# Two tiles of a two-layer kernel: norms and half the bias steps moved from ScalarE to VectorE, and another planned order

## The chip, the cores and the metric

The kernel runs on one core of a Trainium2 chip. A core has five engines, each with its own instruction queue that runs strictly in order: TensorE (PE, matrix products), VectorE (DVE), ScalarE (ACT, table functions), GpSimd (POOL) and SyncE (SP, here the queue from which all transfers are issued). [...] The metric is device microseconds of one execution, the median of several runs.

## The reference

Two layers work on x of 2 sequences x 2048 positions x 256 features. Layer 0 normalizes x, runs a state-space block (projection, a convolution of four taps, softplus, a scan over time with 16 states for each of 512 channels, gating, projection, a residual and a GELU feed-forward), and multiplies it with the SiLU of a gated network whose weights and activations are quantized to 4-bit floats. Layer 1, the part that the change touches, is cut here to what matters:

```python
xn = layernorm(x)
# attention over the two sequences (their axis is the attended one)
s = out_proj(softmax(q @ k.T * scale) @ v) + out_proj_bias
h = xn                                    # three low-rank-corrected blocks
for blk in range(3):
    y = qlora_linear(h, 2*blk)            # x W^T + bias + (x A^T) B^T
    y = layernorm(y) * gamma + beta
    y = gelu(y)
    h = qlora_linear(y, 2*blk+1) + h
x = x + s * silu(h)
```

All arithmetic is float32.

## The kernel before

**Tiling.** The positions of a sequence are cut into 8 pieces of T = 256; with B = 2 sequences that gives 16 steps (j, b). A step has the stages HEAD (norm, input projection, convolution, softplus), QUANT (`fp4_half`, the gated network), SCAN (16 states, each one: ScalarE makes four 128x256 `decay` tiles, VectorE multiplies, scans 1028 columns and multiplies again, TensorE adds the transposed result into a `bank_y`), and TAIL (norm and feed-forward, then `x1`). After the second sequence's step of each j comes SECOND: `second(j, g, x1)` for g = 0, 1 does layer 1 on 128 positions of both sequences. There are 16 such tiles. The two of the last j have streams of their own, `e0` and `e1`, with other buffers and PSUM banks (`bank_m`, `bank_y`, `bank_h`, `bank_f`), since nothing else is left by then; all others are `s0` and `s1`.

**A tile of layer 1.** `second` (line 1100) takes the statistics of x1 on VectorE, gets the inverse root on GpSimd (`inverse_root`, line 705: a tensor_scalar and a power), normalizes on ScalarE, transposes on TensorE, does the attention (over two elements it is a sigmoid), and then walks three blocks k = 0, 1, 2. A block is: TensorE makes `py`; ScalarE squares it with a running sum, twice (the weights had their mean taken out, so the mean of squares is the variance); GpSimd makes `y`; ScalarE scales twice; TensorE transposes; ScalarE applies Gelu; TensorE adds the second product to `hb`; ScalarE adds the bias, in two halves m (k = 2 applies SiLU instead). The lines, of before:

```python
rec.scalar.activation(yn[:, bb, :], py[:, bb, :], AF.Square, accum_out=sq[:, bb : bb + 1])
y = inverse_root(st, sq, B, 1.0 / D, EPS, f"f{nm}_{k}")
rec.scalar.activation(yn[:, bb, :], py[:, bb, :], AF.Copy, scale=y[:, bb : bb + 1])
```

**What sets the order.** No operation is issued where it is written. `Recorder` keeps all of them with what they read and write, and a planner in the program's build (`order`, `forward`, `backward`) walks them with a cost for each (`cost`, line 104), a delay from one engine's end to another's start (`SEEN`, `TAIL`), the number of buffers of every tag, and a price for switching ScalarE's function table (`SWITCH`). `forward` always issues the ready operation with the highest key. The first keys come from the step number, a `lead` for each stage and the table `adjust` of (step, stage, shift); then each row of `passes` walks back from the end for due times and forward again with these as keys. What it finds is the order in which the instructions stand in the five queues. The chip doesn't see the planner's times: it sees only the queues and their semaphores. Since the whole plan follows from these numbers, a changed cost or shift moves instructions everywhere. ScalarE's table loads are put in by the compiler wherever the next function is not in the table that is loaded, so their number follows from the order, too.

All operations are issued from one line (561), so the profile is read by the names of the tiles. `hh`, `decay`, `state`: scan. `fp_l`, `fp_h`, `h`, `hq`: quantized network. `t2k_s`, `ln_y_s`, `bank_s`: layer 1's tiles; in the last two also `bank_m`, `bank_y`, and `lnt`, `ux` and `dt` as their working tiles.

Of the kernel before, what the change touches and what calls it, by code (L numbers as in the profile page):

```python
# [8 lines left out]
F32 = mybir.dt.float32  # L9
I32 = mybir.dt.int32  # L10
BF16 = mybir.dt.bfloat16
AF = mybir.ActivationFunctionType
ALU = mybir.AluOpType
AX = mybir.AxisListType
PSUM = bass.MemoryType.PSUM
DRAM = bass.MemoryType.DRAM

P = 128
D = 256
# [3 lines left out]
T = 256  # L23
# [13 lines left out]
EPS = 1e-5  # L37
# [4 lines left out]
class Recorder:  # L42
# [11 lines left out]
    SWITCH = 1.31  # L54

    SEEN = {"tensor": 0.055, "vector": 0.034, "scalar": 0.035, "gpsimd": 0.1, "sync": 0.07}
    TAIL = {"tensor": 0.165, "vector": 0.083, "scalar": 0.1, "gpsimd": 0.8, "sync": 1.7}

    WINDOW, COLUMNS = 3.4133, 3060
    RATE = 165e3  # L60
# [43 lines left out]
    def cost(self, engine, method, args, kwargs):  # L104
        out = kwargs.get("out", args[0] if args else None)
        n = 1
        for d in out.shape[1:]:
            n *= d
        if engine == "sync":
            return 0.52  # L110
        if engine == "gpsimd":
            if method == "memset":
                return 0.04
            return 0.7 if method == "tensor_tensor" else 0.3
        values = list(args[1:]) + list(kwargs.values())
        tiles = [v for v in values if hasattr(v, "tensor") and v is not out]
        if engine == "tensor":
            rhs = args[2] if len(args) > 2 else kwargs.get("rhs")
            if method == "transpose" or kwargs.get("is_transpose"):
                return 0.109  # L120
            if rhs.dtype == BF16:
                return 0.1 + n / 2400.0
            lhs = kwargs.get("lhsT", args[1] if len(args) > 1 else None)
            if lhs.shape[0] == 16 and lhs.offset >= 16 * lhs.ap[0][0]:
                return 0.1
            return 0.005 + 4 * n / 2400.0
        scalars = 0
        for v in tiles:
            m = 1
            for d in v.shape[1:]:  # L130
                m *= d
            scalars += m == 1 and n > 1
        if engine == "scalar":
            inside = bool(tiles) and self.space(tiles[0].tensor) == PSUM
            scalars += kwargs.get("accum_out") is not None
            return (0.05 if inside else 0.093) + 0.000833 * n + 0.1 * scalars
        if method == "tensor_tensor_scan":
            return 0.068 + 0.002083 * n
        if method == "bn_stats":
            return 0.333  # L140
        if method == "bn_aggr":
            return 0.1
        if method == "reciprocal":
            return 0.06 + 0.0066 * n
        if method == "tensor_reduce":
            n = 1
            for d in args[1].shape[1:]:
                n *= d
        if method in ("tensor_copy", "tensor_scalar", "memset") and n >= 64:
            return 0.07 + 0.00052 * n + 0.06 * scalars  # L150
        if n <= 32:
            return 0.078
        return 0.067 + 0.0010417 * n + (0.06 if method == "scalar_tensor_tensor" and scalars else 0.0)
# [47 lines left out]
    def prepare(self):  # L201
# [12 lines left out]
        for i, (engine, method, args, kwargs, stage) in enumerate(ops):  # L214
            if engine == "tensor":

                n = self.costs[i]
                lhs = kwargs.get("lhsT", args[1] if len(args) > 1 else None)
                if method == "transpose" or kwargs.get("is_transpose"):
                    self.size[i], self.table[i] = 128, 1  # L220
                elif lhs.dtype == BF16:
                    self.size[i], self.table[i] = (n - 0.1) * 2400, 2
                else:
                    self.size[i], self.table[i] = n * 2400 * lhs.shape[0] / 128, 3
            if engine == "sync":
                self.size[i] = 2 if args[0].dtype == BF16 else 4
                for d in args[0].shape:
                    self.size[i] *= d
# [28 lines left out]
    def order(self, lead, bonus, ahead, adjust=(), passes=()):  # L257

        own = {(b, k): v for b, k, v in adjust}
        key = [-o[4][0] - lead[o[4][1]] + own.get(o[4], 0.0) for o in self.ops]
        issued, end = self.forward(key, bonus, ahead)
        for unit, bonus_back, ahead_back, bonus, ahead, adjust in passes:
            key = [-x / unit for x in self.backward(unit, bonus_back, ahead_back)]
            for b, k, v in adjust:
                for i, o in enumerate(self.ops):
                    if o[4] == (b, k):
                        key[i] += v  # L270
            issued, end = self.forward(key, bonus, ahead)
        return issued, end

# [78 lines left out]
    def forward(self, key, bonus, ahead):  # L352
# [65 lines left out]
        while done < n:  # L418
# [25 lines left out]
            for name in self.first[i]:  # L444
                if name not in place:
                    t = max(t, tags[self.tiles[name]["tag"]]["free"][0][0])
            cost = costs[i]
            if best_e == "scalar" and table[i] and table[i] != now_table:
                t = max(t, free[best_e] + self.SWITCH)
                self.switched += self.SWITCH  # L450
                now_table = table[i]
# [113 lines left out]
def tile_two_layers(ctx: ExitStack, tc: tile.TileContext, a: dict):  # L565
# [139 lines left out]
    def inverse_root(stream, v, n, scale, plus, name):  # L705

        y = small.tile([P, n], F32, tag=f"ln_y_{stream.replace("e", "s")}", name=f"y_{name}")
        rec.gpsimd.tensor_scalar(y, v, scale, plus, ALU.mult, ALU.add)
        rec.gpsimd.tensor_tensor(y, y, power[:, :n], ALU.pow)
        return y  # L710

# [73 lines left out]
    wt = {}  # L785
# [78 lines left out]
    def head(b, j, xt):  # L864
# [57 lines left out]
            rec.sync.dma_start(bc[q * NS : (q + 1) * NS, :], xdbl[(2 * q + 1) * R : (2 * q + 2) * R, :])  # L922
        dt = mam.tile([P, 4, T], F32, tag="dt", name=f"dt_{nm}")
        ux = mam.tile([P, 4, T], F32, tag="ux", name=f"ux_{nm}")
        pdt = [bank("m", f"pdt_{nm}_{pr}").rearrange("p (m t) -> p m t", m=2) for pr in range(2)]
        for mm in range(2):
            for pr in range(2):
                rec.tensor.matmul(
# [171 lines left out]
    def second(j, g, x1):  # L1100
        nm = f"{j}_{g}"

        st = f"e{g}" if j == NJ - 1 else f"s{g}"
        xv = x1[:, g, :, :]
        xm = t2k(st, f"xm_{nm}").rearrange("p (b d) -> p b d", b=B)
        layer_norm(st, xm, xv, B, f"c{nm}")

        hb = bank({"s": "h", "e": "g"}[st[0]] + st[1], f"hb_{nm}").rearrange("p (c t) -> p c t", c=2)
        for c in range(2):
# [63 lines left out]
        for k in range(3):  # L1173
# [8 lines left out]
                    )  # L1182
            yn = t2k(st, f"yn_{nm}_{k}").rearrange("p (b d) -> p b d", b=B)

            sq = small.tile([P, B], F32, tag=f"ln_sq_{st.replace("e", "s")}", name=f"sq_{nm}_{k}")
            for bb in range(B):
                rec.scalar.activation(
                    yn[:, bb, :], py[:, bb, :], AF.Square, accum_out=sq[:, bb : bb + 1]
                )
            y = inverse_root(st, sq, B, 1.0 / D, EPS, f"f{nm}_{k}")  # L1190
            for bb in range(B):
                rec.scalar.activation(yn[:, bb, :], py[:, bb, :], AF.Copy, scale=y[:, bb : bb + 1])
            pt = transpose_pair(st, yn, f"e{nm}_{k}")
            yt = t2k(st, f"yt_{nm}_{k}").rearrange("p (c t) -> p c t", c=2)
            for c in range(2):
# [10 lines left out]
                    )  # L1206
            hn = t2k(st, f"hn_{nm}_{k}").rearrange("p (c t) -> p c t", c=2)
            for m in range(2):
                rec.scalar.activation(
                    hn[:, m, :], hb[:, m, :], AF.Identity if k < 2 else AF.Silu,  # L1210
                    bias=wt["odd"][:, k, m : m + 1],
                )
# [20 lines left out]
    for i, (j, b) in enumerate(order):  # L1233
# [20 lines left out]
        h = following  # L1254

    adjust = [
        (0, 0, 1.48), (0, 2, 0.93), (0, 3, -0.66), (1, 0, -1.29), (1, 1, -0.08), (1, 3, 0.49),
        (1, 4, -0.55), (2, 0, -0.28), (2, 1, 0.62), (2, 4, 0.73), (3, 0, -0.1), (3, 4, 0.51),
        (4, 0, 0.15), (4, 1, 0.67), (4, 2, 0.59), (4, 3, -1.78), (4, 4, -0.74), (5, 0, -0.51),
        (5, 2, 0.63), (5, 3, 0.09), (5, 4, 0.29), (6, 0, 0.66), (6, 1, 1.68), (6, 2, 0.9),  # L1260
        (6, 3, 0.26), (6, 4, 2.72), (7, 0, 0.63), (7, 1, -0.41), (7, 2, 0.3), (7, 4, 0.34),
        (8, 0, -0.58), (8, 1, -0.58), (8, 2, 0.45), (8, 3, 0.6), (8, 4, -0.47), (9, 0, 0.76),
        (9, 1, 2.32), (9, 2, -0.12), (9, 4, -0.53), (10, 0, 0.19), (10, 3, 2.6), (10, 4, 0.12),
        (11, 0, 0.54), (11, 1, -0.16), (11, 2, -0.01), (11, 3, -0.3), (11, 4, 1.13),
        (12, 0, -0.62), (12, 1, 0.85), (12, 2, 0.08), (12, 4, 0.47), (13, 0, 0.34),
        (13, 1, -0.42), (13, 2, -1.48), (13, 4, -0.77), (14, 0, -1.31), (14, 1, 0.5),
        (14, 2, -1.21), (14, 3, -1.46), (14, 4, 0.39), (15, 1, 1.91), (15, 2, -0.55),
        (15, 3, 1.48), (15, 4, 0.61),
    ]


    passes = [
        (110, 0.3, 0.0, 0.5, 0.12, [(9, 0, 0.01)]),
        (110, 0.3, 0.1, 0.5, 0.12, [(9, 0, 0.01)]),
        (80, 0.3, 0.0, 0.2, 0.12, []),
        (30, 0.3, 0.05, 0.5, 0.05, []),
        (20, 0.3, 0.1, 0.5, 0.12, []),
        (20, 0.3, 0.1, 0.5, 0.12, [(3, 4, 0.16)]),
    ]
    rec.issue(tc, lead=(0.28, -1.79, 0, -5.22, 1.4), bonus=366.531, ahead=0, adjust=adjust, passes=passes)  # L1280


# [46 lines left out]
```

## Time and profile before

| | us |
|---|---|
| median of 3 runs (1790.72 to 1791.84) | 1791.33 |
| the profiled execution: its own time | 1787.97 |
| the profiled execution: span, first to last instruction | 1786.2 |
| VectorE busy, of the span | 1630.4 (91%) |
| TensorE busy | 1585.8 (89%) |
| ScalarE busy | 1559.0 (87%) |
| of it 383 table loads | 491.4 |
| GpSimd busy | 233.2 (13%) |
| mean granted TensorE clock | 0.947 |

How to read it: in the groups, a row is an engine, an operation, what it writes and reads, the number of instructions, busy time and mean ns, and after the second bar the idle time just before them with what ended it. In the waits, "A <- B: 15.2, 14, 3.5" says that A's engine stood idle 15.2 us in 14 places, 3.5 at most, until B. In the timeline, a row is start, duration, engine, operation, with the idle time before it in brackets. Busy time of neighbouring instructions on one engine overlaps by some hundredths of a microsecond.

### The profile page before, as it was taken

How to read it: one execution, taken by the hardware profiler on the slowest of the kernel's cores; microseconds unless marked ns; L12 is line 12 of the kernel's file. 1: busy time of each engine (PE TensorE's matmuls, PEld its weight loads, DVE VectorE, ACT ScalarE, POOL GpSimd, SP SyncE). 2: the span in 40 equal slices, each digit the busy share in tenths (PEclk: the TensorE clock that was granted, in tenths of full speed). 3: DMA queues.
4: the chain of work that ended last, by engine and by line, in shares of the span. 5: the costliest groups of instructions: out<-in, count | busy, mean ns of one | idle time of the engine just before them, and what ended most of it. 6: DMA issues, size and time to landing. Idle time of an engine off the chain costs nothing.

```text
span 1786.2 us, 22221 instructions
## 1 busy us (share of the span) xinstructions
PE 1585.8 (89%) x7756; PEld 1193.1 (67%) x7756; DVE 1630.4 (91%) x1926; ACT 1559.0 (87%) x3324; POOL 233.2 (13%) x265
## 2 busy tenths in 40 slices
PE   7448878999989989899998999999899999998887
PEld 5336656677776768676776767767676767766665
DVE  7999999999989999999998999999998999999711
ACT  7556968899988999989998999999999998999645
POOL 1000010022122201211111021101111102020101
PEclk9669989899999999999999999999999999999989
DMA  6311111111111111212121212211111111212000
GB/s 180 92 41 45 48 43 59 42 45 46 45 48 45 48 49 48 60 36 49 41 61 38 52 43 54 54 31 53 43 60 37 48 49 44 46 36 64 2 6 12
DMA packets 62989, 86.77 MB, mean 49 GB/s; under 512 B 15095, under 2 KB 29085, under 8 KB 62878
## 3 DMA queue, kind: packets, MB, share of 16 engines
q1 hardware_dynamic: 62878, 85.37, 17.9%
q8 instruction: 60, 0.98, 0.2%
q14 instruction: 51, 0.42, 0.1%
HBM read 80.62 MB, written 4.72 MB: 48 GB/s over the span
## 4 chain that ended last, share of the span: by engine, by line
ACT 41%; PE 32%; DVE 19%; issue 5%; POOL 2%; DMA 0%; ACTq 0%; DVEq 0%
ACT L561 14%; PE bank_f L561 13%; ACT decay L561 11%; DVE hh L561 10%; PE bank_m L561 7%; ACT t2k_s L561 6%; PE bank_s L561 5%; PE bank_y L561 4%; DVE fp_l L561 3%; ACT t2k_f L561 3%; PE bank_h L561 2%; POOL ln_y_s L561 2%; ACT xc L561 1%; DVE t2k_s L561 1%; DVE fp_sc L561 1%
## 5 line engine op out<-in xcount | busy, mean ns | idle before, releaser
L561 DVE TENSOR_TENSOR_SCAN hh<-decay,hh 128x1028 f32<-128x1028 f32 x256 | 581.4, 2286 | 5.7 <-ACT decay L561 4.4
L561 ACT ACT_TABLE_LOAD x383 | 491.4, 1283 | 13.9 <-DMA xt<-in_x_dram 3.7
L561 ACT ACTIVATE decay<-dt,amat 128x256 f32<-128x256 f32 x1024 | 445.0, 500 | 6.4 <-DVE hh L561 3.3
L561 PE MATMUL bank_y<-ident,hh 128*128 128x128 f32 x2048 | 296.5, 284 | 30.8 <-DVE hh L561 30.6
L561 DVE TENSOR_TENSOR hh<-hh,bcs 128x1024 f32<-128x1024 f32 x256 | 308.4, 1210 | 15.9 <-ACT state L561 15.2
L561 DVE TENSOR_TENSOR hh<-ux,bcs 128x1024 f32<-128x1024 f32 x256 | 307.5, 1210 | 1.7 <-PE bank_y L561 1.6
L561 PEld LDWEIGHTS bank_y<-ident,hh 128*128 128x128 f32 x2048 | 248.7, 146 | 82.3 <-DVE hh L561 43.1
L561 PE MATMUL bank_f<-w_f,t2k_f 128*128 128x256 f32 x512 | 133.7, 388 | 14.1 <-ACT t2k_f L561 14.0
L561 POOL TENSOR_SCALAR ln_y_s<-ln_sq_s 128x2 f32<-128x2 f32 x48 | 36.9, 769 | 769.8 <-ACT t2k_s L561 458.1
L561 PE MATMUL bank_m<-xi,cdiag 128*128 128x256 f32 x512 | 127.0, 380 | 0.0
L561 PE MATMUL bank_f<-t2k_f,w_f 128*128 128x256 f32 x512 | 124.6, 384 | 2.5 <-ACT t2k_f L561 2.5
L561 PEld LDWEIGHTS bank_f<-w_f,t2k_f 128*128 128x128 f32 x512 | 92.8, 192 | 36.0 <-ACT t2k_f L561 23.5
L561 PE MATMUL bank_f<-w_down,hq 128*128 128x256 f32 (+1 forms) x384 | 103.7, 409 | 7.3 <-ACT hq L561 7.2
L561 PEld LDWEIGHTS bank_f<-t2k_f,w_f 128*128 128x128 f32 x512 | 94.9, 190 | 21.0 <-ACT t2k_f L561 7.1
L561 PE MATMUL bank_h<-t2k_s,w_l 128*128 128x256 f32 x360 | 95.2, 399 | 9.5 <-ACT t2k_s L561 9.2
L561 PEld LDWEIGHTS bank_m<-xi,cdiag 128*128 128x128 f32 x512 | 93.0, 190 | 14.1 <-issue 0.7
L561 DVE SCALAR_TENSOR_TENSOR fp_l<-fp_h,fp_l 128x704 f32<-128x704 f32 (+2 forms) x124 | 91.4, 737 | 7.5 <-ACT fp_h L561 6.9
L561 PE MATMUL bank_f<-ident,fp_l 128*128 128x128 f32 x292 | 54.5, 311 | 47.1 <-DVE fp_l L561 46.5
L561 PE MATMUL bank_f<-w_gate,t2k_f 128*128 128x352 f32 x256 | 92.7, 481 | 2.2 <-ACT h L561 1.1
L561 PEld LDWEIGHTS bank_f<-w_down,hq 128*128 128x128 f32 (+1 forms) x384 | 71.8, 199 | 34.1 <-issue 12.7
L561 POOL TENSOR_TENSOR ln_y_s<-ln_y_s,power 128x2 f32<-128x2 f32 x64 | 93.2, 1457 | 5.2
L561 PE MATMUL bank_f<-w_up,t2k_f 128*128 128x352 f32 x256 | 90.2, 466 | 0.0
(187 smaller groups left out, 2589.9 us busy)
## 6 DMA issues: line engine op xcount, KB each, us to landing
bcs<-bc SPq DMA_DIRECT2D x128, 512.0 KB, 4.8
xt<-in_x_dram SPq DMA_DIRECT2D x16, 256.0 KB, 2.8
out_dram<-t2k_s SPq DMA_DIRECT2D x15, 256.0 KB, 3.8
w_f<-in_ffn_w_dram SPq DMA_DIRECT2D x2, 1024.0 KB
t2k_s<-in_qweights_dram SPq DMA_DIRECT2D x6, 256.0 KB, 2.9
w_in<-in_in_proj_w_dram SPq DMA_DIRECT2D x1, 1024.0 KB
h<-in_w_gate_dram SPq DMA_DIRECT2D x6, 128.0 KB, 2.1
w_qkv<-in_qkv_w_dram SPq DMA_DIRECT2D x1, 768.0 KB
```

What stands on the lines that cost most here:

```text
L561: getattr(getattr(self.nc, engine), method)(*args, **kwargs)
```

## The change

1. For the two last tiles (`last`, streams e0 and e1): the first norm's normalization goes from ScalarE to VectorE (one tensor_scalar, subtract and multiply, for each sequence); the norms in the three blocks take `statistics` on VectorE (bn_stats and bn_aggr) instead of Squares on ScalarE, and scale with one VectorE tensor_tensor over 512 columns instead of two ScalarE copies; the scale-and-add ahead of the power goes from GpSimd to VectorE; and of the two bias steps of k = 0 and 1, the half m = 1 goes to VectorE.
2. The planner's costs: GpSimd's operations 0.69 and 0.19 rather than 0.7 and 0.3, its delay 0.3 rather than 0.8, and its operations (memset aside) start only when VectorE's current call is over; float32 products of fewer than 192 columns cost as 192; a ScalarE call with a running sum and a VectorE call that reads PSUM cost more.
3. New `lead`, `adjust`, `passes`, `bonus` and `ahead`; `adjust` in a pass may name an engine. The order of all queues differs.

In the built queues VectorE has 1972 instructions instead of 1928, ScalarE 3204 instead of 3230, among them 389 table loads instead of 383, GpSimd 262 instead of 270; TensorE's and SP's are as many as before, in another order.

```diff
-    TAIL = {"tensor": 0.165, "vector": 0.083, "scalar": 0.1, "gpsimd": 0.8, "sync": 1.7}
+    TAIL = {"tensor": 0.165, "vector": 0.083, "scalar": 0.1, "gpsimd": 0.3, "sync": 1.7}
...
-            return 0.7 if method == "tensor_tensor" else 0.3
+            return 0.69 if method == "tensor_tensor" else 0.19
...
-            return 0.005 + 4 * n / 2400.0
+            return 0.005 + 4 * max(n, 192) / 2400.0
...
-            scalars += kwargs.get("accum_out") is not None
+            scalars += 1.5 * (kwargs.get("accum_out") is not None)
...
+            if tiles and self.space(tiles[0].tensor) == PSUM:
+                return 0.067 + 0.0010417 * n + 0.06 * scalars
...
+            if engine == "gpsimd":
+                self.table[i] = int(method != "memset")
...
+            if best_e == "gpsimd" and table[i]:
+                t = max(t, free["vector"])
...
-        rec.gpsimd.tensor_scalar(y, v, scale, plus, ALU.mult, ALU.add)
+        if stream[0] == "e":
+            rec.vector.tensor_scalar(y, v, scale, plus, ALU.mult, ALU.add)
+        else:
+            rec.gpsimd.tensor_scalar(y, v, scale, plus, ALU.mult, ALU.add)
         rec.gpsimd.tensor_tensor(y, y, power[:, :n], ALU.pow)
...
-        layer_norm(st, xm, xv, B, f"c{nm}")
+        if last:
+            mv = statistics(st, xv, B, f"c{nm}")
+            y = inverse_root(st, mv[:, :, 1], B, 1.0, EPS, f"c{nm}")
+            for i in range(B):
+                rec.vector.tensor_scalar(
+                    xm[:, i, :], xv[:, i, :], mv[:, i, 0:1], y[:, i : i + 1], ALU.subtract, ALU.mult
+                )
+        else:
+            layer_norm(st, xm, xv, B, f"c{nm}")
...
+            if last:
+                mv = statistics(st, py, B, f"f{nm}_{k}")
+                y = inverse_root(st, mv[:, :, 1], B, 1.0, EPS, f"f{nm}_{k}")
+                rec.vector.tensor_tensor(
+                    yn, py, y.unsqueeze(2).to_broadcast([P, B, D]), ALU.mult
+                )
+            else:
...
+                if last and m == 1 and k < 2:
+                    rec.vector.tensor_scalar(
+                        hn[:, m, :], hb[:, m, :], wt["odd"][:, k, m : m + 1], None, ALU.add
+                    )
+                    continue
...
-    rec.issue(tc, lead=(0.28, -1.79, 0, -5.22, 1.4), bonus=366.531, ahead=0, adjust=adjust, passes=passes)
+    rec.issue(tc, lead=(2.87, -2.69, 0, -5.2, 0.74), bonus=2058732.142, ahead=0.015, adjust=adjust, passes=passes)
```

## The prediction

> **What bounds the kernel now.** I read the totals, then busy time by stage, then the waits before the last scan, then the timeline of the last two tiles. By stage (length, then each engine's busy us, granted clock, DMA share, GB/s):
>
> ```profile
> PE 1585.8 (89%) x7756; PEld 1193.1 (67%) x7756; DVE 1630.4 (91%) x1926; ACT 1559.0 (87%) x3324; POOL 233.2 (13%) x265
> ...
> 0.00:100.00 100.00, 59.42 (x256) 42.66 (x256) 86.00 (x192) 60.56 (x133) 9.62 (x32) 0.79 0.48 127
> ...
> 300.00:1600.00 1300.00, 1217.72 (x6054) 921.23 (x6053) 1248.23 (x1405) 1222.09 (x2623) 194.48 (x176) 0.97 0.18 47
> ...
> 1676.00:1717.00 41.00, 40.13 (x198) 31.43 (x196) 12.86 (x31) 25.60 (x50) 2.81 (x8) 1.00 0.00 1
> 1717.00:1740.50 23.50, 18.91 (x62) 11.10 (x63) 5.23 (x13) 9.48 (x16) 1.67 (x4) 0.78 0.03 11
> 1740.50:1786.20 45.70, 33.53 (x145) 23.66 (x144) 5.63 (x11) 24.48 (x66) 5.30 (x12) 0.94 0.03 12
> ```
>
> VectorE's last scan product ends at 1675.2 us. Up to 1676 it idles only 69 us: 14 in the first 100, 52 between 300 and 1600, where ScalarE idles 78. So time before 1675 is VectorE's work plus what the order makes it wait. From 1676 to 1717 TensorE is full (40.1 of 41). After 1717 nobody is full: two tiles walk one chain from engine to engine. The waits of VectorE and ScalarE before 1676 (us, times, longest):
>
> ```profile
> DVE hh L561 <- ACT state L561: 15.2, 14, 3.5
> ...
> DVE fp_l L561 <- ACT fp_h L561: 5.8, 7, 3.1
> DVE hh L561 <- ACT decay L561: 4.4, 6, 1.8
> ...
> DVE xi L561 <- PE bank_m L561: 2.7, 1, 2.7
> ...
> DVE ln_m_m L561 <- POOL ln_y_m L561: 2.5, 3, 1.4
> ...
> DVE ln_m_f L561 <- POOL ln_y_f L561: 1.8, 2, 1.2
> ```
>
> ```profile
> ACT t2k_s L561 <- POOL ln_y_s L561: 9.7, 6, 3.6
> ```
>
> All waiting for GpSimd's roots is thus 4.3 us on VectorE and 9.7 on ScalarE: the whole purse that better planning of GpSimd can open there. Two groups price the rest:
>
> ```profile
> L561 ACT ACT_TABLE_LOAD x383 | 491.4, 1283 | 13.9 <-DMA xt<-in_x_dram 3.7 <-PE bank_h L561 2.3 <-DVE hh L561 1.9
> ...
> L561 POOL TENSOR_TENSOR ln_y_s<-ln_y_s,power 128x2 f32<-128x2 f32 x64 | 93.2, 1457 | 5.2
> ```
>
> GpSimd's power takes 0.69 us in the tail, 1.46 on average. In the tail, ScalarE in one step of tile e0:
>
> ```profile
> 1755.25 0.38 ACT L561 ACTIVATE t2k_s<-bank_m 128x256 f32<-128x256 f32 x1
> ...
> 1757.74 0.47 ACT L561 ACTIVATE t2k_s<-bank_m,ln_y_s 128x256 f32<-128x256 f32 x1
> 1759.57 0.38 ACT L561 ACTIVATE lnt<-bank_y 128x256 f32<-128x256 f32 x1 [1.35 <-PE bank_y L561]
> ...
> 1760.30 0.48 ACT L561 ACTIVATE t2k_s<-bank_m,ln_y_s 128x256 f32<-128x256 f32 x1
> 1761.42 1.02 ACT L561 ACTIVATE t2k_s<-bank_m,l_bet,l_gam 128x256 f32<-128x256 f32 x2 [0.64 <-PE bank_m L561]
> ```
>
> The second half of e0's scaling stands behind e1's Square, which waits for TensorE: 2.1 us lost in the queue, not in arithmetic.
>
> **The change part by part.** The sum is made against the profiled execution: span 1786.2, its own time 1787.97, 3.4 below the median 1791.33 of the three runs. I apply the difference to the median. "Work ahead" below is the built queue, each instruction at its group's mean less the overlap with its neighbour.
>
> *Tail, the norms.* Removed from ScalarE: 12 Squares (0.38 + 0.20), 12 scalings (0.47), 4 normalizations (0.59), 4 bias steps (0.47), together 17 us; from GpSimd 8 tensor_scalars (0.19). Added to VectorE: 12 statistics (0.41), 12 aggregates (0.17), 8 small scale-and-add (about 0.15, as the 128x44 row at 0.18), 6 scalings (0.68, the row of bank_s + x at 128x512), 4 normalizations (unseen; 0.27 for a 128-wide one with a scalar, 0.475 from PSUM at 256: I take 0.40), 4 bias steps (0.475), less two 0.15: some 16 us, in a stretch where VectorE is busy 5.23 of 23.5 and 5.63 of 45.7. Per norm the chain itself doesn't shorten: old 0.84 + 0.09 + 0.96 + 0.1 + 0.82 = 2.8; new 0.75 + 0.29 + 0.15 + 0.69 + 0.69 and four hand-overs = 2.8. What goes is the queueing on ScalarE. e0's projections end at 1740.5, 1754.7 and 1768.3: 14.2 and 13.6 apart, while TensorE's work for both tiles in a step is 2 x (0.31 + 1.72 + 0.6 + 1.72) = 8.7. Bounds: only the halved bias steps count (4 x 0.36 = -1.4), or both steps fall to TensorE's 8.7 and the front gains 2.6: -13. Following the new queues from the end of e0's first projection: scaled at 2.65 (1.05 + 0.15 + 0.7 + 0.7 with hand-overs), transposed 3.3, Gelu 4.3, second product 6.0, bias 6.5; then TensorE still has e1's projection (1.7) and the rest of e1's output product (1.3) ahead of e0's next: 11.5; the next step likewise gives about 10.5. That is -6, of which half a microsecond per step may go in hand-overs. To this come 1.7 to 2.6 at the front, where VectorE normalizes right after the former tile's product instead of handing to ScalarE (1721.7 to 1723.9 today). Against it: a third Silu/Gelu alternation puts the last load (1.28) after TensorE's last product; the scaling of e0's first norm stands in front of e1's two last attention adds, so these wait out GpSimd's 0.69; TensorE's clock is 0.78 here. I take -7.
>
> *Between the last scan and 1717.* In the new order 37.5 us of TensorE work stands from the last scan's transposes to the end of the FFN; today 33.0, but TensorE starts it 3.5 late. 0 to +4.5; I take +1, since TensorE would start at once.
>
> *The order, VectorE.* Its work ahead of the last scan product is the same (1595.1 against 1594.6 us). So before 1675 only its idle time can move.
>
> *The order, start.* SP now sends the gate weights first and x second: x is one issue (0.5) later, covered by the weights' quantization on VectorE. 41.8 us of VectorE work stand before the first scan (36.6 before) and 20.2 of ScalarE's before its decay (25.3): more filler, an earlier decay. The 14.0 idle is 3.4 unavoidable (DMA and launch). Bounds 0 and -10; I take -3, the two stalls of xi (2.7) and fp_h (3.1) half gone.
>
> *The order, table loads.* 389 instead of 383, five more before the last decay, one in the tail: 5 x 1.283 = +6.4 on ScalarE, and its work ahead of the middle tiles' decays is 5 to 11 us more. ScalarE idles 78 us in that stretch, which may cover it: 0 to +10, I take +3.
>
> The trace has the next ACTIVATE 1.29 after a load starts (1745.67 to 1746.96). [...]
>
> *The order, GpSimd.* Cost figures come nearer to the rows (0.69 and 0.19, and a wait for VectorE). Yet the room on ScalarE between the last Square and the first scaling has the same median, 3.5 us, in both orders. Bounds 0 and -14 (4.3 + 9.7); I take -2. Shape edits (the slice of pdt) change nothing in any queue.
>
> Sum: -7 + 1 - 3 + 3 - 2 = -8: span about 1778, median 1783.3.
>
> **The rivals.** *A, slower: ScalarE falls behind the scans.* It already waits 45.6 us for scans before it can copy a state, and VectorE waits 15.2 + 4.4 for state and decay. With five more loads and up to 11 us more work ahead of the decays, that wait is where the middle breaks. Doubled, it is +19.6: 1803. It decides from a growth of 8. For it: 78 us of ScalarE idle is only 6%; against: its surplus is back to 3.0 us at the last decay.
>
> *B, no difference: the tail doesn't pay.* Chains are equally long, TensorE runs at a low clock, the last load is exposed: tail -2, and start and loads cancel: 1789 to 1791.
>
> *C, a larger gain.* Most of the start's stalls and of the GpSimd waits go: -7 more and -6 more: 1770. For it: the planner's GpSimd costs were far off; against: the equal room named above.
>
> **How the numbers follow.** This kernel's runs spread 1.1 us; 0.2% (3.6 us) is about what can be told from no change. Forecast 0.45 (1776 to 1788), C 0.18, B 0.15, A 0.22. Faster: forecast and C, 0.63; same: B, 0.15; slower: A, 0.22. The range leaves out the ends of A and C: 1768 to 1799.
>
> **What would show it.** Right: the stretch from e0's first to third projection falls from 27.8 to about 22; VectorE's idle before its last scan product is 66 or less; the last product ends near 1673; after it about 105 us remain instead of 111; loads 389 at 1283 ns. Wrong: VectorE's waits for state and decay above 28 us (A); steps of the last tiles still 13 apart (B); the waits for ln_y gone and under 60 us idle (C). The forecast falls first if the middle's idle, which the order sets and no row shows, moves by more than 10 either way.

## The result: slower by half a per cent

The changed kernel takes 1796.8 us, median of 15 runs (1792.19 to 1808.14), beside 1791.16 for the kernel before (15 runs, 1778.83 to 1797.57): ratio 1.0047, 95% interval 1.003 to 1.0064. The ratio is estimated from all runs and isn't the quotient of the medians: these are 5.6 us apart, and a ratio of 1.0047 is 8.4 us. Measured again later, beside other kernels (after_again below), it was 1.0061 (1.004 to 1.0082), some 11 us. The forecast was 8 us faster; the measured time lies in its range (1768 to 1799), on the other side of no change.

The profiled execution of the changed kernel took 1802.07 us (span 1800.3), 14.1 more than the profiled one of before. That is more than the medians differ by: single executions of one kernel spread by some 1% here, and the profiles show it, too, so below a size is taken from several profiles or from the times where there are any. One execution of a kernel below, before_late2, took 3271.71 us and is left out of its ratio (its median is 1785.35 without it, 1786.05 with it).

The page of after, totals and the two groups shown of before:

```profile
PE 1583.1 (88%) x7756; PEld 1198.4 (67%) x7756; DVE 1636.4 (91%) x1970; ACT 1553.3 (86%) x3286; POOL 246.3 (14%) x257
...
L567 ACT ACT_TABLE_LOAD x389 | 499.1, 1283 | 15.3 <-PE bank_h L567 2.9
...
L567 POOL TENSOR_TENSOR ln_y_s<-ln_y_s,power 128x2 f32<-128x2 f32 x64 | 95.6, 1495 | 59.1 <-DVE ln_y_s L567 54.7
```

Busy time hardly moved: the loads are as many and as long as forecast, and the mean of GpSimd's power rose by 38 ns only. The loss doesn't show in any total. By stage, after (columns as in the prediction):

```profile
0.00:100.00 100.00, 60.59 (x262) 43.74 (x262) 83.39 (x201) 55.02 (x122) 9.45 (x31) 0.83 0.48 124
...
1687.10:1736.50 49.40, 48.68 (x225) 37.51 (x223) 14.37 (x36) 27.48 (x58) 4.28 (x8) 0.99 0.00 1
1736.50:1760.10 23.60, 19.58 (x78) 12.92 (x78) 11.26 (x30) 8.96 (x15) 2.04 (x3) 0.93 0.04 12
1760.10:1800.30 40.20, 27.77 (x128) 20.59 (x128) 13.70 (x38) 14.71 (x26) 3.46 (x5) 0.96 0.04 13
```

Three stretches moved. The last scan product ends at 1687.1 instead of 1675.2. From there to the last statistics of x1 (the end of the feed-forward) it takes 49.3 us with TensorE full, where it took 41.8. From there to VectorE's last add it takes 60.6 instead of 65.7. The waits ahead of the last scan product, of VectorE and then of ScalarE:

```profile
DVE hh L567 <- ACT decay L567: 21.0, 17, 6.1
DVE hh L567 <- ACT state L567: 10.5, 11, 2.5
```

```profile
ACT t2k_s L567 <- POOL ln_y_s L567: 25.3, 7, 6.7
```

VectorE's waits for state and decay are 31.5 us (19.6 before), past the 28 that the prediction gave as the sign of rival A. A second profile of the changed kernel (after_again, below) has them shorter, under 28:

```profile
DVE hh L567 <- ACT state L567: 11.8, 12, 2.5
DVE hh L567 <- ACT decay L567: 10.9, 11, 3.4
```

What both profiles share is the wait that the change was to shorten, ScalarE's for the roots: it grew from 9.7 to 25.3 (23.0 in the second). The longest of the waits of the first profile, at GpSimd, VectorE and ScalarE:

```profile
1120.22 2.65 POOL L567 TENSOR_SCALAR ln_y_s<-ln_sq_s 128x2 f32<-128x2 f32 x1 [15.66 <-ACT t2k_s L567]
1122.95 7.75 POOL L567 TENSOR_TENSOR ln_y_s<-ln_y_s,power 128x2 f32<-128x2 f32 x1
```

```profile
1122.80 1.20 DVE L567 TENSOR_TENSOR hh<-hh,bcs 128x1024 f32<-128x1024 f32 x1
...
1125.05 0.68 DVE L567 SCALAR_TENSOR_TENSOR fp_l<-fp_h,fp_l 128x512 f32<-128x512 f32 x1
...
1126.79 1.22 DVE L567 TENSOR_TENSOR hh<-ux,bcs 128x1024 f32<-128x1024 f32 x1
1127.92 2.29 DVE L567 TENSOR_TENSOR_SCAN hh<-decay,hh 128x1028 f32<-128x1028 f32 x1
1130.13 0.67 DVE L567 TENSOR_TENSOR fp_l<-fp_l,fp_sc 128x512 f32<-128x512 f32 x1
1132.79 2.30 DVE L567 TENSOR_TENSOR_SCAN hh<-decay,hh 128x1028 f32<-128x1028 f32 x1 [2.00 <-ACT decay L567]
```

```profile
1130.73 0.84 ACT L567 ACTIVATE t2k_s<-bank_s,ln_y_s 128x256 f32<-128x256 f32 x2 [6.71 <-POOL ln_y_s L567]
```

A power of 0.69 us is out for 7.75, through six VectorE calls, and comes in where the scan of 1127.92 ends. The new planner counts on GpSimd waiting for the one call that is running. ScalarE reaches the scaling at 1124.02, 3.9 us after the last Square, and stands 6.71 us in front of it, with decays queued behind, and VectorE's next scan waits for its decay.

### The profile page after: what moved, and what is told of

It is laid out like the page before. It is cut to its first block, busy times and chain, and to the rows that moved or that the text cites. A ratio compares the mean times of both kernels' runs of the same rounds, so it can differ in the third digit from the quotient of the medians.

```text
span 1800.3 us, 22200 instructions
## 1 busy us (share of the span) xinstructions
PE 1583.1 (88%) x7756; PEld 1198.4 (67%) x7756; DVE 1636.4 (91%) x1970; ACT 1553.3 (86%) x3286; POOL 246.3 (14%) x257
## 4 chain that ended last, share of the span: by engine, by line
ACT 37%; PE 33%; DVE 21%; issue 4%; POOL 3%; DMA 1%; SPq 0%; ACTq 0%; DVEq 0%
PE bank_f L567 13%; DVE hh L567 13%; ACT L567 13%; ACT decay L567 9%; PE bank_m L567 8%; ACT t2k_s L567 5%; PE bank_s L567 5%; PE bank_y L567 5%; DVE fp_l L567 3%; POOL ln_y_s L567 3%; ACT t2k_f L567 2%; PE bank_h L567 2%; DVE t2k_s L567 1%; ACT xc L567 1%; DVE fp_sc L567 1%
## 5 line engine op out<-in xcount | busy, mean ns | idle before, releaser
L567 ACT ACT_TABLE_LOAD x389 | 499.1, 1283 | 15.3 <-PE bank_h L567 2.9
L567 PE MATMUL bank_y<-ident,hh 128*128 128x128 f32 x2048 | 286.0, 282 | 36.1 <-DVE hh L567 35.8
L567 PEld LDWEIGHTS bank_y<-ident,hh 128*128 128x128 f32 x2048 | 244.1, 145 | 84.5 <-DVE hh L567 48.0
L567 POOL TENSOR_SCALAR ln_y_s<-ln_sq_s 128x2 f32<-128x2 f32 x42 | 46.5, 1108 | 690.6 <-ACT t2k_s L567 509.8
L567 PEld LDWEIGHTS bank_f<-t2k_f,w_f 128*128 128x128 f32 x512 | 99.2, 196 | 19.1 <-ACT t2k_f L567 3.6
L567 PE MATMUL bank_f<-ident,fp_l 128*128 128x128 f32 x292 | 51.8, 307 | 46.4 <-DVE fp_l L567 37.9
```

What stands on the lines that cost most here:

```text
L567: getattr(getattr(self.nc, engine), method)(*args, **kwargs)
```

## The experiments

The planner's order is a list. Each experiment takes that list from the unchanged program and exchanges or moves single calls when it is issued (`swap` below maps a call's number to what is issued in its place), so that all other calls keep their places in the queues. The code below is shortened to its sense.

### Tail and order, each alone

```diff
+# tail_alone: order of before; the calls of the old tail replaced, e.g. for a block of e0, e1
+swap[Square(0)] = [vector.bn_stats(0)]
+swap[Square(1)] = [vector.bn_stats(1), vector.bn_aggr(0), vector.bn_aggr(1)]
+swap[gpsimd.tensor_scalar(y)] = [vector.tensor_scalar(y, variance, 1.0, EPS)]
+swap[Copy(0)] = [vector.tensor_tensor(yn, py, y)];  swap[Copy(1)] = []
+swap[Identity(m=1, k<2)] = [vector.tensor_scalar(hn, hb, bias)]
+# order_alone: order of after; the same in the other direction
```

> The order of before, kept call by call, with the last two tiles' norms, scalings and bias steps on VectorE put in at the old calls' places. Theory 1 (the order loses, the tail edit gains): about 5 us faster than before, 1786; from the statistics of x1 to the last add some 60 us instead of 65.7, all ahead of it unchanged (last scan product near 1675, then 42 us). Theory 2 (the shorter last stretch of the changed kernel comes from its new order there, the edit itself gives nothing): within 1.5 us of before, the last stretch 64 to 67.

> The order of the changed kernel, kept call by call, with the last two tiles' norms, scalings and bias steps back on ScalarE and GpSimd at the new calls' places. Theory 1: about 5 us slower than the changed kernel, so 10 to 11 us slower than before, near 1802; VectorE's waits for state and decay stay near 31 us ahead of the last scan product. Theory 2: the time of the changed kernel, 1797, since the order alone makes both the loss and the shorter last stretch.

Measured: tail_alone 1794.3 us beside 1794.74 of before, ratio 1.0005 (0.9989 to 1.0021): nothing. order_alone 1805.02, ratio 1.0074 (1.005 to 1.0097). So the loss is the order's, and theory 1 is half wrong: order_alone lost the 10 us that it forecast, but the edit of the tail isn't worth 5 us in the order of before. In the new order the two measurements of the changed kernel lie 0.27% and 0.13% below order_alone, with overlapping intervals, so no worth of the edit is shown there. The last stretch (from x1's statistics to the last add), one windows line each of before, tail_alone, before_no_root (below; old tail) and after:

```profile
1717.00:1782.70 65.70, 52.43 (x206) 34.76 (x206) 10.87 (x24) 33.97 (x82) 6.97 (x16) 0.90 0.01 4
```

```profile
1727.80:1795.90 68.10, 55.17 (x206) 37.10 (x206) 24.48 (x68) 21.30 (x38) 5.49 (x8) 0.85 0.01 4
```

```profile
1706.50:1775.30 68.80, 55.82 (x206) 37.28 (x206) 10.90 (x25) 33.96 (x82) 7.02 (x16) 0.85 0.01 4
```

```profile
1736.50:1797.10 60.60, 47.35 (x206) 33.50 (x206) 24.96 (x68) 23.68 (x40) 5.49 (x8) 0.97 0.03 9
```

ScalarE lost 12.7 us of busy time in tail_alone (33.97 to 21.30; the forecast's sum of durations was 17), and the stretch didn't get shorter. Read TensorE's column: the same 206 matmul records take 47.4 to 55.8 us, by the granted clock of 0.97 to 0.85, and the stretch is TensorE's time and 13 us in all four, whichever engine makes the norms. Two rows of tail_alone show eight products of one shape, the first time in 3.49 us, at half clock for all but the end by the clock record, the second time in 2.08:

```profile
1757.98 3.49 PE L562 MATMUL bank_y<-w_l,lnt 128*128 128x256 f32 x8
...
1770.56 2.08 PE L562 MATMUL bank_y<-w_l,ux 128*128 128x256 f32 x8 [0.62 <-ACT ux L562]
```

The clock record of the last stretch holds pieces of half clock of 3.4 us or multiples: 13.7 us in before (10.2 from 1719.3 on and 3.4 from 1773.9 on), 20.5 in tail_alone and before_no_root, 3.4 in after; the granted clocks of 0.90, 0.85, 0.85 and 0.97 in the four lines above agree. One order with one tail had 13.7 us of it in one execution and 20.5 in another. What sets the clock at half no run here shows; the longest gap of TensorE in these three stretches and in that of after is 3.0 us.

All profiles by stretch (us; the last column is TensorE's busy time in the last stretch):

| kernel | order, tail | last scan product | to x1's statistics | to the last add | TensorE |
|---|---|---|---|---|---|
| before | old, old | 1675.2 | 41.8 | 65.7 | 52.4 |
| tail_alone | old, new | 1686.0 | 41.8 | 68.1 | 55.2 |
| before_no_root | old, old | 1665.0 | 41.5 | 68.7 | 55.8 |
| before_late (see below) | old, old | 1665.8 | 53.0 | 65.1 | 51.8 |
| before_late2 | old, old | 1670.5 | 41.8 | 65.6 | 52.3 |
| before_late2_tail | old, new | 1676.3 | 41.8 | 68.4 | 55.4 |
| after | new, new | 1687.1 | 49.3 | 60.6 | 47.4 |
| after_again | new, new | 1683.7 | 48.5 | 63.6 | 50.3 |
| order_alone | new, old | 1687.1 | 48.1 | 62.3 | 50.6 |
| after_no_root | new, new | 1659.3 | 49.2 | 60.6 | 47.3 |
| after_late | new, new | 1690.6 | 49.3 | 60.7 | 47.4 |

The first column is noisy: before and tail_alone are the same up to there, and differ by 10.8. The second is not: but for before_late it is 41.5 to 41.8 in the old order and 48.1 to 49.3 in the new. The third varies with the clock, by 3 us between executions with one order and tail (65.7 and 68.7, 60.6 and 63.6). So the new order costs 6 to 8 us in the drain after the scans, and its last stretch is 2 to 8 shorter, with either tail; why TensorE's clock is higher there no run shows.

### Nobody waits for the roots

```diff
+# stream not e0, e1: GpSimd still makes y, nobody reads it
-rec.scalar.activation(yn[:, bb, :], py[:, bb, :], AF.Copy, scale=y[:, bb : bb + 1])
+rec.scalar.activation(yn[:, bb, :], py[:, bb, :], AF.Copy, scale=power[:, bb : bb + 1])
+# the same for normalize(): its product mean * y and its scale
```

> The order of the changed kernel; GpSimd still works out every root, but outside the last two tiles the calls that scale by it read a constant tile (a wrong scale), so nobody there waits for GpSimd. Theory 1 (starved roots hold ScalarE, and so the decays): ScalarE's 25 us of waits for ln_y go, VectorE's waits for state and decay fall from 31.5 to about 20, the last scan product ends 8 to 12 us earlier, time 8 to 12 us below the changed kernel (about 1786). Rival (ScalarE's five more loads and its moved work delay the decays): the waits for state and decay stay above 27 and the time falls by under 4 us.

> The order of before, with the same edit: outside the last two tiles nobody waits for GpSimd's roots (constant scale instead). Theory 1: there is less to win here, since ScalarE waits 9.7 us and VectorE 4.3 for roots: 2 to 5 us faster than before, clearly less than the same edit gives in the changed order. Rival: the same gain in both orders, whatever it is, since then the roots are not what differs.

Measured: after_no_root 1774.12 us, ratio 0.9892 (0.9869 to 0.9916); before_no_root 1779.09, ratio 0.9912 (0.9885 to 0.994). From the changed kernel's 1.0061 that is -1.7%, some 30 us; from before it is -0.9%, some 16. So the roots are what differs between the two orders: 12 to 14 us of difference, by the first or the second ratio of the changed kernel, and known to some 7 us by the intervals. Without them the new order isn't slower any more (a median 5 us lower; the two intervals overlap). The purse was larger than the expectation had it in both, and it is about what the two engines' waits for GpSimd add up to: 30.2 us in the profile of after (25.3 and 4.9; 27.6 in after_again, 28.4 in order_alone), 14.0 in that of before (9.7 and 4.3; 19.0 in tail_alone, with the same order). VectorE's waits behind them, of after_no_root (last scan product at 1659.3), then of before_no_root:

```profile
DVE hh L568 <- ACT decay L568: 5.3, 8, 1.4
...
DVE hh L568 <- ACT state L568: 2.1, 6, 0.5
```

```profile
DVE hh L562 <- ACT state L562: 8.9, 11, 2.1
...
DVE hh L562 <- ACT decay L562: 4.1, 6, 1.8
```

From 31.5 (22.7 in after_again) to 7.4 in the new order, with its 389 loads and its fuller ScalarE queue unchanged. So the loads, to which the prediction gave +3 and rival A its cause, weren't the trouble.

### The same roots' scalings later in the queue

```diff
+LATE = {16: 7, 44: 7, 49: 7, 57: 7, 58: 6, 59: 7, 65: 7, 92: 4, 93: 5, 98: 3}  # after_late: root, calls
+LATE = {16: 7, 22: 5, 29: 7, 35: 7, 100: 7}                                    # before_late
+LATE = {16: 7, 22: 5, 29: 7, 35: 7}                                            # before_late2
+order = self.later(order, LATE)  # the two scalings, and what needs them, behind so many ScalarE calls
```

> The order of the changed kernel, complete, but for ten roots of the second layer (those that GpSimd was held at for over 3.5 us in one of the runs of this order) the two scalings on ScalarE, with the transposes that read them, stand 3 to 7 ScalarE calls later, behind decays and state copies; as many table loads. Theory 1: ScalarE's waits for ln_y_s ahead of the last scan product fall from 25 us to under 6, VectorE's waits for state and decay from 31.5 (26.3 with the old tail) to under 20, time 8 to 15 us below the changed kernel: 1783 to 1790, under the kernel before. Rival (it is not the place of these scalings; the order is short of ScalarE time): the waits move to the next call, time within 4 us of the changed kernel.

> The same move in the order of before, for its five held roots (5 to 7 calls later, two table loads fewer). Theory 1: there is less to win, ScalarE waits some 10 to 14 us for five roots: 3 to 6 us faster than before. Rival: no difference in either order.

> The changed kernel itself beside the others on one chip. Both theories: 0.3 to 0.65% over before, 1796 to 1803; the long holds of GpSimd at the same roots and of the same length as in its first profile, if the order alone makes them; elsewhere and of other lengths if chance does.

Measured on one chip: after_late 1792.72 us, ratio 1.0004 (0.999 to 1.0017); after_again 1803.81, ratio 1.0061 (1.004 to 1.0082); before_late 1795.92, ratio 1.0016 (1.0004 to 1.0027). Ten pairs of calls, moved by a few places, take back 10 us, the whole loss. That is theory 1's size, though the time isn't under the kernel before, as it had it. ScalarE's waits for ln_y_s went from 23.0 (after_again) to 10.0 rather than under 6, and VectorE's for state and decay are 26.4, not under 20: the profiled execution of after_late was its slowest, at 1805.53, so its waits are no measure of the gain in the median. In after_again GpSimd's long holds came back at the same calls with the same length: 6.01, 6.61, 7.75 and 5.92 us at roots 44, 57, 65 and 92 in all three profiles of this order (the last one is of a scale-and-add, the others are powers). order_alone's row for the one shown above:

```profile
1130.98 7.75 POOL L568 TENSOR_TENSOR ln_y_s<-ln_y_s,power 128x2 f32<-128x2 f32 x1
```

So most holds belong to the order; a few others (root 49: 1.59 in after, 7.15 in order_alone and after_again) fall one way or the other. The old order has one power held so long, at root 22, 7.14 to 7.15 us in all six of its profiles.

before_late was expected to gain and lost 0.16%. Its last scan product ended 9.4 us earlier than in before (1665.8), but the next stretch took 53.0 instead of 41.8: its root 100 stands just there, and the moved calls held up TensorE's queue (busy 43.6 us of the 53.0, and 40.9 of 41.8 in before). So the next run left that one in place.

> The order of before with four held roots' scalings 5 to 7 ScalarE calls later; the fifth, which stands in the drain after the last scan, stays where it was (moving it lengthened the stretch from the last scan product to the last statistics from 41.8 to 52.9 us). Theory 1: the last scan product ends 5 to 9 us earlier than in before, as in the former run (1665.8), the drain is back at 42: 1783 to 1787, 0.3 to 0.5% faster than before. Rival: no difference (the earlier last product was chance, the spread of one kernel's profiles being about that).

> The same with the last two tiles' norms, scalings and bias steps on VectorE. If the edit of the tail is worth nothing in this order, as the run of it alone had it: the time of the run without it, within 2 us. If it is worth 5 us once the roots do not hide it: 1778 to 1782.

Measured: before_late2 1786.05 us, ratio 0.9959 (0.9944 to 0.9974), which beats both kernels, and is theory 1's size; before_late2_tail 1786.26, ratio 0.9955 (0.9938 to 0.9972). Four roots' scalings a few calls later are worth 7 us in the order of before, and the tail's edit, on top of it, nothing once more. With held roots moved in both, the new order is still behind the old one (1.0004 and 0.9959). The waits of before_late2, VectorE's and ScalarE's:

```profile
DVE hh L592 <- ACT state L592: 7.2, 10, 1.4
```

```profile
ACT t2k_s L592 <- POOL ln_y_s L592: 2.4, 4, 0.9
```

### What keeps GpSimd out

> No part of the reference: GpSimd's scale-and-add and power on 128x2 (0.19 and 0.69 us when undisturbed) are released at the start of a run of some 10 us of VectorE calls, three times for each kind of run, and nothing else goes on. Theory 1 (a run of calls with two SBUF inputs keeps GpSimd out until the run ends): the pair ends only with the run, 8 to 10 us, beside the multiplies, the scans and the scale-subtract calls, and takes 1 to 2 us beside calls with one input or one input in PSUM. Rival (GpSimd waits for the current call alone, as the new planner has it): each of the two waits at most one call, so the pair takes 2 to 3.5 us beside the multiplies and 3 to 6 beside the scans.

Measured, GpSimd's rows beside multiplies and beside bn_stats:

```profile
17.43 1.55 POOL L71 TENSOR_TENSOR y_mult<-y_mult,power 128x2 f32<-128x2 f32 x1
...
157.25 0.69 POOL L71 TENSOR_TENSOR y_stats<-y_stats,power 128x2 f32<-128x2 f32 x1
```

The rival is right: in this loop GpSimd waits for the running call alone. The pair takes 2.7 us beside multiplies and 4.8 beside scans (2.09 and 2.60), in the middle of a run of 9 to 11 us. With one input in PSUM, or bn_stats, there is no wait (0.19 and 0.69); beside a one-input multiply from SBUF to SBUF the pair takes 1.7 (0.55 and 1.11). The 7.75 above, through six calls, is more than a wait for one.

Over seven profiles (before, after, order_alone, after_again, after_late, before_late, tail_alone) the power's first chance depends on when it starts. Started 0.14 to 0.165 us into a multiply, which is where it comes when the end of the call before let in the scale-and-add, it was still out after that multiply's end in 30 of 81 cases; in 20 of these it came in only where a scan ended, after 4.9 to 8.4 us. Started 0.2 us or later into a multiply: in 0 of 109. Into a scan, at 0.14 to 0.165: 0 of 37. (A multiply here is one that writes `hh`.)

> No part of the reference: GpSimd's pair of root calls released at the start of a scan that one, two, three, four or six multiplies and then another scan follow (also eight multiplies and no scan; five multiplies first; scans alone). Theory (a power released 0.15 us into a multiply, right after a scan's end let the scale-and-add in, stays out at every multiply's end until a scan ends): the power takes about 1.2 us a multiply plus 2.2 for the scan plus 0.5: 3.8 with one, 5 with two, 7.2 with four, 9.5 with six, and 9 or more with eight and no scan. Rival (it waits for the call that is running and no other): 1.6 in all of them, 2.6 beside scans alone.

> No part of the reference: the sequence scan, multiply in place, three more multiplies, two scans, with the kernel's own tile shapes (rows of 257, a broadcast second operand), GpSimd's pair released at the first scan's start; alone, and beside ScalarE's exponentials, TensorE's transposes of the products, broadcast loads, ScalarE's earlier copies into the tiles (so that VectorE's calls carry waits), and all of them. Theory (the hold comes from the shapes and the in-place multiply): the power takes 7.1 us, to the scan's end, in every case. Rivals: only beside the engine that makes it (that case and the one with all), or in no case, 1.6 us, and then what decides between 1.6 and 7.1 in the kernel stays open.

Measured in port_probe2, where the power starts at 0.15 us into the first of four multiplies behind a scan:

```profile
86.16 1.59 POOL L71 TENSOR_TENSOR y_s<-y_s,power 128x2 f32<-128x2 f32 x1
```

It is 1.59 to 1.61 in all 18 cases with a scan in front, and 1.74 to 1.76 in all 21 of port_probe3, whatever else is running there (in that one the power starts 0.03 us into the multiply, so it doesn't repeat the place). The holds of the kernel didn't come about in a loop by itself. What decides between 1.6 and 7 us stays open; that it is so in the kernel, at most of the same calls in profile after profile of an order, is what the traces show.

## Why the prediction was wrong, step by step

**"The order, GpSimd: bounds 0 and -14, I take -2."** This is the step that failed. Everything that waits for roots was summed rightly to 14 us in the trace of before (taking those waits away gave 16), but it was taken as something that the new order could only make smaller. The bound on the other side was missing. Measured: 28 to 30 us in place of 16 by taking the roots' waits away, so +12 to +14 instead of -2. The evidence used, an equal median room of 3.5 us between last Square and first scaling, was read rightly and was no evidence: four waits, of 3.8 to 6.7 us (at roots 57, 65, 92 and 98), make 20.7 of the 25.3. And the room isn't what changed. In the traces ScalarE reaches the scaling 3.7 us (median) after the last Square in before and 3.5 in after, and in front of these four waits it is 3.1 to 4.9. What changed is how long GpSimd takes: from the start of the scale-and-add to the end of the power it is over 7 us for five of layer 1's roots in each of the three profiles of the new order, for one in before and for two in tail_alone, while the median is 2.3 us in before and 2.1 in after. Another order puts other VectorE calls beside the roots, and a hold past the call that is running was in neither the forecast nor the planner's costs. Which of the planner's new numbers brought more long holds isn't shown.

**Rival A** had the right direction and the wrong cause. Its sign, VectorE's waits for state and decay growing by more than 8, came in the first profile (by 11.9) and not in the two others of this order (by 6.7 in order_alone, by 3.1 in after_again), whose kernels lost as much or more. It blamed five loads and 5 to 11 us of work ahead of the decays; with both still there and the roots' waits gone, the waits for state and decay fell to 7.4. Rival C needed the waits for the roots to go; they grew.

**"Table loads +3"**: 389 loads at 1283 ns, as forecast. No run shows that the six more cost anything; after 375 of the 383 loads of before the next call starts within 1.35 us of the load's start.

**"Between the last scan and 1717: 0 to +4.5, I take +1, since TensorE would start at once."** Measured +6 to +8, outside the bounds. The 37.5 us of TensorE work were counted from the last scan's transposes on; but in the new order quantized products and products of layer 1 still stand in front of these, and the transposes start about 6 us after the last scan product (1689.9 against 1683.7 in after_again), with TensorE busy all along. Work in front of the mark belonged to the sum.

**"Tail, the norms: -7."** The stretch became shorter by 5.1 in the first pair of profiles, and e0's first to third projection takes 24.7 us (from the starts of their statistics, 1755.2 and 1779.9) instead of 27.8, forecast 22; that looks like the forecast. But the edit alone gave 0.05% slower (-0.1% to +0.2%), and by the ends of the projections these two steps take 24.2 us with the old tail in the new order (order_alone) and 30.5 with the new tail in the old order (tail_alone, at a clock of 0.81 in the first step). So the order made them shorter. The edit did so by no more than about half a microsecond: less the 3.4 us that the half clock cost there, 30.5 is 27.1 (an estimate), and before has 27.7. The term that failed is TensorE's work in a step, summed to 8.7 us for both tiles. Here are the two steps in before:

```profile
1740.70:1754.70 14.00, 11.62 (x54) 8.05 (x53) 2.86 (x7) 8.30 (x22) 1.77 (x4) 1.00 0.00 1
1754.70:1768.30 13.60, 11.38 (x52) 8.09 (x51) 0.00 (x0) 8.09 (x24) 1.77 (x4) 1.00 0.00 0
```

TensorE is busy 11.6 and 11.4 us in them, at full clock, since other products of e1 stand there too; 4.6 us of the two steps could go at most, where the forecast took 6 and held over 10 possible. The queueing on ScalarE was real, and didn't set the pace. The clause "TensorE's clock is 0.78 here" stood among the things against, without a size; it is worth 3 us from one execution to another. Rival B ("the tail doesn't pay, TensorE runs at a low clock") had this part.

**"The order, VectorE: its work ahead of the last scan is the same"**: right. VectorE's durations up to there add up to 1734.6 us, 1737.9 before; only idle time moved, as the prediction said it would have to (it is idle 90.0 us up to there, 69.3 before; the forecast had 66 or less; 86.2 in after_again, and 79.3 in tail_alone, which has the order of before).

**"Start -3"**: VectorE's busy time in the first 100 us is 83.4 against 86.0 (81.8 in after_again, 82.5 in order_alone; 80.1 in tail_alone, which has the order of before). Nothing gained; the spread is as large as the step.

**"This kernel's runs spread 1.1 us"** came from three runs; fifteen span 18.7. A difference of 3.6 us couldn't be told from single profiles, and the sum was made against one.

Together: roots +12 to +14 and drain +7 make about +20; the measured +5.6 to +10.9 leave some -10 to -15 for the rest. The pair without roots has that rest, too: in its profiles the last scan product ends 5.7 us earlier in the new order, the drain is 7.7 longer and the last stretch, with the clock of these executions, 8.1 shorter. No run divides it further, so the terms are known to a few us each.

## What to carry to other kernels

Waits that an order can shorten it can lengthen as well: give such a term both signs, and look at the few longest waits, since a median says nothing of them. Before work is moved off an engine in a chain of several engines, divide the stretch by the busy time of each: here it was TensorE's time and 12 to 13 us in eleven profiles, and 12.7 us less work on ScalarE didn't shorten it. And where a planner sets the order, try moving a handful of calls in the order that is there before planning anew: four pairs of calls gave 7 us, a new plan lost 6 to 11.

## What the runs showed of the hardware

A GpSimd call of 0.69 us was held through as many as six VectorE calls in a row (in after 4.88 us from 1620.34 on, through three, and 7.75 from 1122.95 on, through six; 4.9 to 8.4 in the 20 cases of seven profiles above), mostly at the same calls in every profile of one order, though in port_probe2 and port_probe3 a run of the same kinds of calls held it for one call only (1.59 to 1.61 and 1.74 to 1.76 us). In the last stretch (60.6 to 68.8 us) TensorE's clock was at half in pieces of 3.4 us or multiples; their sum, 3.4 to 20.5 us over eleven profiles (granted clock 0.97 to 0.85), differs between executions of one order with one tail, and the stretch was 3 us longer with the larger sum (65.7 and 68.7 us, 60.6 and 63.6).
